# Two graph layers by two-level Strassen products on one core: the norms' shift on GpSimd, T1 of y out of PSUM, joint sums for P7 and P4, a last pair at full width, and new orders

## The chip, the cores and the metric

The kernel runs on one core of a Trainium2 chip. The time is device microseconds of that core, from one launch. A core has TensorE (PE in the profile, with PEld for its weight loads), VectorE (DVE), ScalarE (ACT), GpSimd (POOL) and SyncE (SP, which here issues every DMA). They run side by side, each in its own order, and meet through semaphores. SBUF is the working memory; PSUM, eight banks of 512 f32 columns by 128 partitions, takes the products.

## The reference

There are 64 graphs of 256 nodes with 512 features each, and an adjacency matrix for each graph, all f32.

```python
# layer 0
deg = sum(adj, -1);  agg = (adj @ x) / max(deg, 1e-6)
x = layernorm(x + relu(concat([x, agg], 2) @ W.T))
# layer 1
q, k = split(x @ Wqk);  v = x @ Wv
w = mask / sqrt(512) * sum(q * (adj @ (k * mask)), -1)      # one score a node
x = layernorm(x + softmax(w over the nodes) * v)
```

A layer norm takes mean and variance over the 512 features. In the kernel `(adj @ x) @ W2.T` becomes `adj @ (x @ W2.T)`, and the two weights of q and k are multiplied with each other once, so that a layer is one product of x with two weight blocks (own part and y, or q and v) and one product of the adjacency with a 256x512 matrix, the gather.

## The kernel before

Graphs are worked in pairs; `NP` is 32. All matmuls are f32. A matmul of 128x128 by n columns is two instructions in the profile.

**The outer products.** The product of a pair's x (transposed, `xT` for layer 0 and `x1T` for layer 1) with the weights is cut into 2x2 blocks and done with seven block products P1 to P7 instead of eight (Winograd's form). `outer_sums`, `fourth_sums` and `weight_sums` make the sums S1 to S4 of x and T1 to T4 of the weights. A product at full width (`outer`) is four matmuls of 512 columns for the pair.

**The inner products.** The products named in `INNER`, all but P6, are cut once more (`inner`, L551 on): seven matmuls of 256 columns. Their sums of x, four rows by three slots in the tile `xT_i` or `x1T_i`, are made by `inner_sums` on GpSimd (L512); `SLOTS_X` says which product uses which slot, and so which product has to be done before another's sums can be made. Each inner matmul lands in one half of a work bank `w`, and has to be taken out before that half is used again: ScalarE copies it to the small tile `fifth` or to the bank of the product, and VectorE adds it. These instructions stand in the profile as ACT `fifth<-bank` and DVE `bank<-bank,fifth`.

**The gather.** `sums_T` (L628) makes T1 to T4 of the 256x512 matrix, `adj_sums` the sums of the adjacency, and `gather` does seven products of two matmuls. In layer 0 its matrix is y, and the sums go to the tile `tv`; P3 ends in the bank y, and `r` in `layer0` copies it to SBUF, 512 columns for each graph of the pair, ahead of `sums_T`. `b11` and `b12` there are the two halves of that copy.

**The norms.** `norm_parts` (L708) gives three parts: ScalarE's mean and squares, then the factor (logarithm and exponential on ScalarE, then `shift = less * rstd`, 128x2, on VectorE), then ScalarE's `own<-own,shift,rstd`. Two norms a graph pair and layer, one for each graph.

**What sets the order.** The loop over pairs runs layer 0 of pair j beside layer 1 of pair j - 1. The order of the matmuls' groups is written out by letters: `ORDER0`, `ORDER1`, `ORDER` for j = 0, 1 and above, `ORDER9` for layer 1 of the last pair, which has no other pair beside it. Lower case is layer 0 and upper case layer 1: `i k m p q r s` and `J K H Q N P L` are products (i and J: P1; k and N: P5; m and K: P2; p and H: P6; q and Q: P7; r and L: P3; s and P: P4), `a` to `g` and `A` to `G` are gathers, and each letter stands for the next matmul group of its product. `HOME` and `HOME9` say which PSUM bank each of them works in. `take` (L890) walks the letters, and `when` starts other work, such as `inner_sums`, once given products are complete. Nothing is issued on the way: `Recorder` notes every operation in a `Plan`, and at the end `Plan.order` (L182) lists the steps of all five engines by a cost model, with due times that come from the place of the dependent matmuls in the letters. So an edit of a cost, an engine or a letter can move any instruction of any engine. Every operation of DVE, ACT and POOL has the line of the recorder, L285, and every matmul L370; they are told apart by their tiles.

**Pairs at the ends.** `FULL_FIRST` leaves P7 and P4 of layer 1 at full width for the first pair. After the loop the last pair's layer 1 runs alone, with `turn_here` for the transposes, `softmax_last` and two norms by halves.

Of the kernel before, what the change touches and what calls it, by code (L numbers as in the profile page):

```python
# [23 lines left out]


INNER = (("P1", "P2", "P5", "P3", "P4", "P7"), ("P1", "P2", "P5", "P3", "P4", "P7"))
SLOTS_X = {"P1": 0, "P2": 1, "P5": 2, "P3": 2, "P6": 0, "P7": 1, "P4": 0}
SLOTS_X1 = {"P1": 0, "P2": 1, "P5": 2, "P6": 0, "P7": 1, **({"P3": 2, "P4": 0} if "P7" in INNER[1] else {"P3": 0, "P4": 1})}
W1_BY_GP = ("P5", "P3", "P4")
HOME = "i6 k7 m7 p0 q6 r7 s6 a7 b2 c3 J3 K2 H5 Q5 N7 L6 P7 A6 B4 C5"  # L30
HOME9 = "J7 K6 H4 Q6 N7 L7 P0 A2 B3 C1"
LATE = 4.0
FULL_FIRST = ("P7", "P4")
ORDER0 = ("i k k i i i i i k i k k m m m k p m k p m p m m r p q r q q q r r r r q q r q s s s s s a b s s "
          "d e c f g")
ORDER1 = ("i k k i i k i k i k i i p m m k k m m p m m p p r r m q q r q r q q r q r q r s s s a J s J s s "
          "J s b J d J J e c J H f H K K H H K g Q K K K K Q N P C A N B Q D N E Q N G N F N N L L P L P L "
          "P L L")
ORDER = ("k k k k i i i L i i i i k m k p k m m p m m q r p p m r r m q q q q q q s s r r s r r s a J s J "
         "J s s b d e J g J c f J J K H K H K K H K K K H A N Q Q Q N Q N Q Q N D N C E Q F P P P G P B N "  # L40
         "P N L P L P L L L L")
ORDER9 = ("J J J J J J J C A D K K E B K K H F G K H Q N H N K H K N N N Q Q Q Q Q N Q P N L P P L L P P P "
          "L P S L Z L L")


class Step:
# [254 lines left out]
class Side:  # L301
# [11 lines left out]
    def chunk(self, s, k, e):  # L313
        return self.block(s)[:, k, e]

    def first_row(self, k, e):
        return self.a[:, k, :, e, 0]


@with_exitstack  # L320
def resnorm_kernel(
# [139 lines left out]
        mm(bank.rearrange("p (a n) -> p a n", n=P), ones,  # L461
           ones[:, None, :].to_broadcast([P, F // P, P]), start=True)

    waiting_sums = {}

    def weight_sums(w, name, layer, by_gp=()):
        b11, b21, b12, b22 = (w[:, k * H:(k + 1) * H, :] for k in range(4))
        t1, t2, t4 = (mem.tile([P, H, F], F32, name=f"{name}{k}") for k in (1, 2, 4))
        it = [mem.tile([P, len(INNER[layer]), HF], F32, name=f"{name}i{r}") for r in (1, 2, 4)]
        sides = {"P1": b11, "P2": b21, "P3": b22, "P4": t4, "P5": t1, "P6": t2, "P7": b12}  # L470
        sub = vec.tensor_sub

        def inner_of(p, b, later=None):
            later = layer == 1 and p in FULL_FIRST if later is None else later
            if p not in INNER[layer]:
                return
            n = INNER[layer].index(p)
            sub = gp.tensor_sub if p in by_gp else vec.tensor_sub
            c11, c12, c21, c22 = (b[:, e, h * HF:(h + 1) * HF] for e in range(2) for h in range(2))
            i1, i2, i4 = (i[:, n] for i in it)  # L480
            if later:
                waiting_sums[p] = lambda: inner_of(p, b, False)
                return
            sides[p] = {"B11": c11, "B21": c21, "B22": c22, "T3": c12, "T1": i1, "T2": i2, "T4": i4}
            sub(i1, c12, c11)
            sub(i2, c22, i1)
            sub(c12, c22, c12)
            sub(i4, c21, i2)
        sub(t1, b12, b11)
        inner_of("P1", b11)  # L490
        sub(t2, b22, t1)
        inner_of("P5", t1)
        sub(b12, b22, b12)
        sub(t4, b21, t2)
        inner_of("P2", b21)
        inner_of("P6", t2)
        inner_of("P7", b12)
        inner_of("P3", b22)
        inner_of("P4", t4)
        return sides  # L500
# [10 lines left out]

    def inner_sums(X, p, eng=gp):  # L512

        if p is None:
            a = [X.first_row(k, e) for k in range(2) for e in range(2)]
            i = [X.i[:, r, 0:2] for r in range(4)]
        else:
            a = [X.chunk(BLOCK[p], k, e) for k in range(2) for e in range(2)]
            i = [X.i[:, r, X.slots[p]] for r in range(4)]
        for to, op, c, d in ((i[0], OP.add, a[2], a[3]), (i[1], OP.subtract, i[0], a[0]),  # L520
                             (i[2], OP.subtract, a[0], a[2]), (i[3], OP.subtract, a[1], i[1])):
            eng.tensor_tensor(to, c, d, op=op)
# [105 lines left out]
    def sums_T(val, to=None):  # L628
        b11, b12, b21, b22 = (val[:, :, t, h * HF:(h + 1) * HF] for t in range(NT) for h in range(2))
        if to is None:  # L630
            tv = ring("tv", [P, 3, 2, HF])
            t1, t2, t4 = (tv[:, r] for r in range(3))
            t3 = b12
        else:
            t1, t2, t4, t3 = (to[:, :, t, h * HF:(h + 1) * HF] for t in range(NT) for h in range(2))
        vec.tensor_sub(t1, b12, b11)
        vec.tensor_sub(t2, b22, t1)
        vec.tensor_sub(t3, b22, b12)
        vec.tensor_sub(t4, b21, t2)
        return {"B11": b11, "B21": b21, "B22": b22, "T1": t1, "T2": t2, "T3": t3, "T4": t4}  # L640

# [63 lines left out]
                onto(1, 0, u)  # L705
        return dict(zip(names, ([u1], [g2], [g5], [u2], [u3], [g3], [u4])))

    def norm_parts(src, total, n=NT):  # L708
        rstd, shift, less, var = (small(x, [P, n]) for x in ("rstd", "shift", "less", "var"))

        def squares():
            act.activation(less, total, AF.Copy, scale=-1.0 / F)
            for t in range(n):
                junk = ring("junk", [P, F], 1, BF16)
                act.activation(junk, src[:, t], AF.Square, bias=less[:, t:t + 1], accum_out=var[:, t:t + 1])

        def factor():
            act.activation(rstd, var, AF.Ln, bias=eps, scale=1.0 / F)
            act.activation(rstd, rstd, AF.Exp, scale=-0.5)
            vec.tensor_tensor(shift, less, rstd, op=OP.mult)  # L720

        def scale(t):
            act.activation(src[:, t], src[:, t], AF.Identity, bias=shift[:, t:t + 1], scale=rstd[:, t:t + 1])
        return squares, factor, scale
# [115 lines left out]
    def layer0(j, X, o, u, y, at):  # L840

        own, yt = owns[j], ys[j]
        make = lambda p, w, q, done, onto=None: product(0, p, X, W0, w, q, done, onto)
        return {
            "i": make("P1", at["i"], u, lambda k: act.copy(own[:, k, 0], u[k])),
            "k": make("P5", at["k"], y, lambda k: act.copy(yt[:, k, 1], y[k])),
            "m": make("P2", at["m"], o, lambda k: act.copy(own[:, k, 0], o[k]), own[:, :, 0]),
            "p": make("P6", at["p"], u, lambda k: vec.tensor_add(yt[:, k, 0], u[k], yt[:, k, 1])),
            "q": make("P7", at["q"], u, lambda k: vec.tensor_add(yt[:, k, 1], u[k], yt[:, k, 1])),
            "r": make("P3", at["r"], y, lambda k: act.copy(yt[:, k, 0], y[k]), yt[:, :, 0]),  # L850
            "s": make("P4", at["s"], u, lambda k: act.copy(own[:, k, 1], u[k])),
        }

# [73 lines left out]
    for j in range(NP):  # L927
# [9 lines left out]
        def when(done, work):  # L937
            waiting.append((full(done, sizes), work))
# [34 lines left out]
            degrees(j + 1)  # L973
        when("k", lambda: (fourth_sums(X), x_sums("P3")))
        when("i", lambda: x_sums("P6"))
        when("m", lambda: x_sums("P7"))
        when("p" if "P6" in INNER[0] else "i", lambda: x_sums("P4"))
        when("pqr", start_gather0)
        when("rs", next_x)
        when("abcdefg", end_gather0)  # L980
# [2 lines left out]
        else:  # L983
# [29 lines left out]
                                    aggs[j - 1]))  # L1013
            when("L" if j > 1 else "m", start_layer1)
            when("J", lambda: y_sums("P6"))
            when("K", lambda: y_sums("P7" if "P7" in INNER[1] else "P4"))
            when("H", lambda: (fourth_sums(Y), y_sums("P4" if "P7" in INNER[1] else "P3")))
            if "P7" in INNER[1]:
                when("HN", lambda: y_sums("P3"))
            T = []  # L1020
            when("ikmpqrs" if j == 1 else "", lambda: T.append(sums_T(owns[j - 1], aggs[j - 1])))
            when("gK", start_gather1)
# [9 lines left out]
    X, x1 = x1Ts[j], owns[j]  # L1032
    turn_here(X, x1, 0, pf)
    take("L " * len(ahead), {"L": ahead}, Counter(), [])
    softmax(j - 1)
    aggs[j] = agg_of(j)
    T = sums_T(x1, aggs[j])
# [6 lines left out]
    at = homes(HOME9)  # L1044
    units, dots = layer1(j, X, q_at, o, u, y, at)
    units.update(gather("ABCDEFG", sumsM.pop(j), T, at["A"], at["C"], at["B"], aggs[j]))
    units["L"] = inner("P3", X, W1, at["L"], y, onto=vs[j][:, :, 0])
    last = []

    def sums(*ps):  # L1050
# [13 lines left out]
    def divide():  # L1064
# [1 line left out]
            last[k](pw[k])  # L1066

    units.update(S=[exps], Z=[divide])
    seven = "P7" in INNER[1]
    sizes = {name: len(parts) for name, parts in units.items()}  # L1070
    waiting = [(full(done, sizes), work) for done, work in (
        ("AB", lambda: (outer_sums(X, vec), sums("P5"))),
        ("J", lambda: sums("P6")),
        ("K", lambda: sums("P7" if seven else "P4")),
        ("H", lambda: (fourth_sums(X), sums("P4" if seven else "P3"))),
        ("HN", lambda: sums("P3") if seven else None),
        ("BFK", dots))]
    take(ORDER9, units, Counter(), waiting)
    p = small("probs", [P, 2, NT], 2)
# [10 lines left out]
    for k in range(2):  # L1090
        total = small("total2", [P, 1], 2)
        stt(k, 1, vs[j][:, k, 1], accum_out=total)
        squares, factor, scale = norm_parts(x1[:, k, 1:2], total, 1)
        squares()
        factor()
        scale(0)
# [34 lines left out]
```

## Time and profile before

| | |
|---|---|
| median of 3 runs | 1842.4 us (1842.38 to 1844.39) |
| profiled execution | 1842.84 us, span 1841.0 us |
| granted TensorE clock | 0.997 |
| PE busy | 1818.4 us, 99% of the span |
| DVE busy | 1672.4 us, 91% |
| ACT busy | 1332.0 us, 72% |
| POOL busy | 1269.4 us, 69% |
| DMA | 181.75 MB, mean 99 GB/s |

Busy time is the time in which an engine has an instruction; the rest of the span it waits. A row of a group names the line, the engine, the operation, the tile written and those read, the shapes, the count, and then the busy time and the mean duration of one. A row of a timeline begins with the start in microseconds from the span's start and the time taken, and ends, in brackets, with the idle time before it and what ended it. A row of a window gives its length and then, for each engine, busy time and number of instructions; then come the clock, the share of the DMA engines and GB/s. Matmuls overlap in the pipe, so their own durations say little, and their starts are what to compare.

### The profile page before, as it was taken

The page shows a single profiled execution, that of the slowest core. Times are in us where ns is not written, and L with a number is a line of the kernel's source. Part 1 is how long each engine was busy: PE and PEld are TensorE (multiplying, and loading weights), DVE is VectorE, ACT ScalarE, POOL GpSimd, SP SyncE. Part 2 cuts the span into 40 slices and gives each one's busy share as a digit, 9 for nine tenths or more (in the row PEclk, how much of TensorE's full clock was granted, in tenths as well). Part 3 has the DMA queues.
Part 4 walks back from the last instruction along what each step waited for, and adds up shares of the span by engine and source line. Part 5 has one row for each costly group of instructions (what it writes and reads, how often), then busy time and mean ns, then how long its engine had stood idle before and what let it go on. Part 6 is the DMA issues. An engine that isn't in the chain of part 4 may idle for free.

```text
span 1841.0 us, 28183 instructions
## 1 busy us (share of the span) xinstructions
PE 1818.4 (99%) x7754; PEld 1433.2 (78%) x7754; DVE 1672.4 (91%) x3627; ACT 1332.0 (72%) x3491; POOL 1269.4 (69%) x1864
## 2 busy tenths in 40 slices
PE   9999999999999999999999999999999999999996
PEld 5767878878778778778778788787787787787785
DVE  7888999999999999999999999999999999999986
ACT  3657876778766778767778767787667787677775
POOL 6876676766676866767766767666768667677652
PEclk9999999999999999999999999999999999999998
DMA  7133333443343343334333334433334333343311
GB/s 247 41 75 102 100 87 98 110 109 94 89 103 102 98 108 100 81 102 118 99 100 102 87 99 110 107 96 88 102 104 99 106 101 81 100 118 100 100 22 64
DMA packets 380733, 181.75 MB, mean 99 GB/s; under 512 B 263712, under 2 KB 345248, under 8 KB 380576
## 3 DMA queue, kind: packets, MB, share of 16 engines
q1 hardware_dynamic: 380576, 179.94, 36.1%
q8 instruction: 63, 1.03, 0.2%
q14 instruction: 94, 0.77, 0.1%
HBM read 114.35 MB, written 34.08 MB: 81 GB/s over the span
## 4 chain that ended last, share of the span: by engine, by line
PE 96%; DVE 2%; ACT 1%; DMA 0%; issue 0%; POOL 0%; SPq 0%; ACTq 0%; DVEq 0%
PE bank L370 96%; DVE own L285 1%; DMA shared<-wqk_t 0%; DVE bank L285 0%; ACT own L285 0%; SPq L386 0%; PE bank L376 0%; DVE tv L285 0%; DVE shared L285 0%; DVE y L285 0%; POOL xT_s L285 0%; DVE w L285 0%; DVE turn L285 0%; DVE x L285 0%; ACT adj L285 0%
## 5 line engine op out<-in xcount | busy, mean ns | idle before, releaser
L285 DVE TENSOR_TENSOR bank<-bank,fifth 128x256 f32<-128x256 f32 x886 | 394.6, 467 | 56.8 <-ACT fifth L285 28.9
L285 ACT COPY fifth<-bank 128x256 f32<-128x256 f32 x632 | 226.9, 376 | 249.0 <-PE bank L370 248.5
L370 PE MATMUL bank<-t_i,x1T_i 128*128 128x256 f32 x760 | 213.2, 382 | 0.4 <-DVE bank L285 0.3
L285 ACT COPY shared<-bank 128x512 f32<-128x512 f32 x314 | 182.4, 595 | 39.9 <-PE bank L370 35.7
L285 POOL TENSOR_TENSOR x1T_i<-x1T 128x256 f32<-128x256 f32 (+1 forms) x188 | 102.5, 552 | 154.9 <-PE bank L370 151.4
L370 PE MATMUL bank<-t_i,xT_i 128*128 128x256 f32 x768 | 205.6, 383 | 1.3 <-POOL xT_i L285 0.9
L285 POOL TENSOR_TENSOR sa<-adj 128x256 f32<-128x256 f32 x128 | 107.4, 839 | 143.1 <-ACT adj L285 136.5
L285 DVE SCALAR_TENSOR_TENSOR own<-bank,rdeg,own 128x256 f32<-128x256 f32 x384 | 170.6, 478 | 27.5 <-PE bank L370 23.9
L285 ACT COPY bank<-bank 128x256 f32<-128x256 f32 (+1 forms) x352 | 148.5, 423 | 62.8 <-DVE bank L285 32.6
L285 ACT ACTIVATE junk<-own,less 128x512 bf16<-128x512 f32 x254 | 185.2, 729 | 3.1
L285 ACT ACTIVATE own<-own,shift,rstd 128x512 f32<-128x512 f32 x254 | 186.7, 810 | 0.4 <-DVE shift L285 0.4
L370 PEld LDWEIGHTS bank<-t_i,xT_i 128*128 128x128 f32 x768 | 142.5, 189 | 43.4 <-ACT bank L285 8.9
L285 ACT COPY y<-bank 128x512 f32<-128x512 f32 x256 | 144.6, 588 | 40.8 <-PE bank L370 39.0
L370 PEld LDWEIGHTS bank<-t_i,x1T_i 128*128 128x128 f32 x760 | 139.9, 189 | 43.5 <-issue 16.1
L370 PE MATMUL bank<-t,x1T_s 128*128 128x512 f32 (+1 forms) x384 | 168.2, 521 | 0.0
L285 DVE TENSOR_TENSOR shared<-bank,shared 128x512 f32<-128x512 f32 (+1 forms) x157 | 140.8, 897 | 25.6 <-PE bank L370 23.1
L370 PE MATMUL bank<-t,xT_s 128*128 128x512 f32 (+1 forms) x384 | 163.5, 521 | 0.1
L370 PE MATMUL bank<-w,x1T_i 128*128 128x256 f32 x508 | 148.9, 384 | 3.1 <-DVE bank L285 1.7
L285 ACT COPY own<-bank 128x512 f32<-128x512 f32 x192 | 112.5, 587 | 47.7 <-PE bank L370 46.8
L370 PE MATMUL bank<-w,xT_i 128*128 128x256 f32 x512 | 143.0, 383 | 0.6 <-DVE bank L285 0.6
L285 POOL TENSOR_TENSOR xT_i<-xT 128x128 f32<-128x128 f32 (+1 forms) x188 | 103.0, 548 | 54.3 <-PE bank L370 42.7
L285 DVE SCALAR_TENSOR_TENSOR own<-own,x 128x512 f32<-128x512 f32 x128 | 131.8, 1033 | 0.0
(173 smaller groups left out, 4805.9 us busy)
## 6 DMA issues: line engine op xcount, KB each, us to landing
x<-x SPq DMA_DIRECT2D x64, 512.0 KB, 3.5
xT<-x_t SPq DMA_DIRECT2D x62, 512.0 KB, 3.5
out<-own SPq DMA_DIRECT2D x62, 512.0 KB, 3.8
x1T<-turn SPq DMA_DIRECT2D x480, 64.0 KB, 2.1
adj<-adj_t SPq DMA_DIRECT2D x64, 256.0 KB, 2.9
turn<-adj SPq DMA_DIRECT2D x64, 256.0 KB, 3.4
turn<-dram SPq DMA_DIRECT2D x31, 264.0 KB, 5.2
shared<-wqk_t SPq DMA_DIRECT2D x4, 512.0 KB, 8.2
```

The costliest lines, as they stand in the source:

```text
L285: self.plan.record(self.name, lambda: call(out, *args, **kwargs), outs, ins, busy, done, port)
L370: plan.record("PE", lambda: nc.tensor.matmul(ps, a, b, start=start, stop=True, skip_group_check=True), [ps], [a, b], busy, busy + 0.165, w ...
```

## The change

- `norm_parts` makes the shift on GpSimd; the last two half norms keep it on VectorE.
- `r` of layer 0 copies only the left half of each y on ScalarE, and VectorE subtracts this half from the right half in PSUM. So the right half of the tile holds T1 when `sums_T` begins, which then makes T2, T3 = T2 - B11 and T4, three subtractions instead of four.
- The sums for the inner products P7 and P4 are made together, four instructions of 256 columns instead of eight of 128. P7 moves to slot 0 and P4 to slot 1, next to each other, and both start when P1 and P2 are done. The first layer 1, with both at full width, has none.
- In the last pair's layer 1, P7, P4 and P3 are done at full width. Three subtractions on GpSimd give those weight blocks back. P3 adds onto the bank of P5, to which VectorE has added the part of v; `after_p5` takes the place of `add_p5`.
- The four orders and both tables of banks are new.

```diff
-SLOTS_X = {"P1": 0, "P2": 1, "P5": 2, "P3": 2, "P6": 0, "P7": 1, "P4": 0}
+SLOTS_X = {"P1": 0, "P2": 1, "P5": 2, "P3": 2, "P6": 0, "P7": 0, "P4": 1}
+SLOTS_X1 = SLOTS_X
-HOME = "i6 k7 m7 p0 q6 r7 s6 a7 b2 c3 J3 K2 H5 Q5 N7 L6 P7 A6 B4 C5"
-HOME9 = "J7 K6 H4 Q6 N7 L7 P0 A2 B3 C1"
+HOME = "i6 k7 m7 p2 q6 r7 s6 a7 b2 c3 J3 K2 H1 Q5 N7 L7 P7 A6 B4 C5"
+HOME9 = "J1 K7 H3 Q7 N6 L1 P1 A2 B3 C1"
+FULL_LAST = ("P7", "P4", "P3",)
-ORDER = ("k k k k i i i L i i i i k m k p k m m p m m q r p p m r r m q q q q q q s s r r s r r s a J s J "
-         "J s s b d e J g J c f J J K H K H K K H K K K H A N Q Q Q N Q N Q Q N D N C E Q F P P P G P B N "
-         "P N L P L P L L L L")
+ORDER = ("i k i i i k k i k i k i k m k p p p m m q m m r p r r m m r r r q q r q q q J q s J J s s s J J "
+         "s a b d s s J e c J H f K K H K H g K K H K K Q Q A N Q N Q Q D N N C Q Q N P N E P N P P G P P "
+         "P L F L B L L L L L")
...
-        if p is None:
-            a = [X.first_row(k, e) for k in range(2) for e in range(2)]
+        if p in (None, "P7P4"):
+            a = [X.row(k, e, int(p is not None)) for k in range(2) for e in range(2)]
...
-            t1, t2, t4 = (tv[:, r] for r in range(3))
-            t3 = b12
+            t2, t3, t4 = (tv[:, r] for r in range(3))
+            t1 = b12
...
+        if to is None:
+            vec.tensor_sub(t3, t2, b11)
+        else:
+            vec.tensor_sub(t3, b22, b12)
...
-            vec.tensor_tensor(shift, less, rstd, op=OP.mult)
+            by.tensor_tensor(shift, less, rstd, op=OP.mult)
...
+        def split(to, ps):
+            act.copy(to[:, :HF], ps[:, :HF])
+            vec.tensor_sub(to[:, HF:], ps[:, HF:], to[:, :HF])
-            "r": make("P3", at["r"], y, lambda k: act.copy(yt[:, k, 0], y[k]), yt[:, :, 0]),
+            "r": make("P3", at["r"], y, lambda k: split(yt[:, k, 0], y[k]), yt[:, :, 0]),
...
-        when("m", lambda: x_sums("P7"))
-        when("p" if "P6" in INNER[0] else "i", lambda: x_sums("P4"))
+        when("im", lambda: inner_sums(X, "P7P4"))
...
+    for p in FULL_LAST:
+        gp.tensor_sub(W1[p]["T3"], W1[p]["B22"], W1[p]["T3"])
+        W1[p] = whole[1, p]
...
+    def after_p5(k):
+        vec.tensor_add(v[:, k, 1], y[k], v[:, k, 1])
+        vec.tensor_add(y[k], y[k], v[:, k, 0])
+    units["N"] = product(1, "P5", X, W1, at["N"], y, after_p5)
+    units["L"] = [go for k in range(2) for go in outer(y, k, X, BLOCK["P3"], W1["P3"])]
```

More of the change, by code (lines that the diff above doesn't have):

```diff
@@ L26 @@
 INNER = (("P1", "P2", "P5", "P3", "P4", "P7"), ("P1", "P2", "P5", "P3", "P4", "P7"))
-SLOTS_X = {"P1": 0, "P2": 1, "P5": 2, "P3": 2, "P6": 0, "P7": 1, "P4": 0}
-SLOTS_X1 = {"P1": 0, "P2": 1, "P5": 2, "P6": 0, "P7": 1, **({"P3": 2, "P4": 0} if "P7" in INNER[1] else {"P3": 0, "P4": 1})}
+SLOTS_X = {"P1": 0, "P2": 1, "P5": 2, "P3": 2, "P6": 0, "P7": 0, "P4": 1}
+SLOTS_X1 = SLOTS_X
 W1_BY_GP = ("P5", "P3", "P4")
-HOME = "i6 k7 m7 p0 q6 r7 s6 a7 b2 c3 J3 K2 H5 Q5 N7 L6 P7 A6 B4 C5"
-HOME9 = "J7 K6 H4 Q6 N7 L7 P0 A2 B3 C1"
+HOME = "i6 k7 m7 p2 q6 r7 s6 a7 b2 c3 J3 K2 H1 Q5 N7 L7 P7 A6 B4 C5"
+HOME9 = "J1 K7 H3 Q7 N6 L1 P1 A2 B3 C1"
 LATE = 4.0
+FULL_LAST = ("P7", "P4", "P3",)
 FULL_FIRST = ("P7", "P4")
[L34 to L38, printed above, removed]
-ORDER = ("k k k k i i i L i i i i k m k p k m m p m m q r p p m r r m q q q q q q s s r r s r r s a J s J "
-         "J s s b d e J g J c f J J K H K H K K H K K K H A N Q Q Q N Q N Q Q N D N C E Q F P P P G P B N "
-         "P N L P L P L L L L")
-ORDER9 = ("J J J J J J J C A D K K E B K K H F G K H Q N H N K H K N N N Q Q Q Q Q N Q P N L P P L L P P P "
-          "L P S L Z L L")
+ORDER0 = ("k i i i k i i i i p k k k k m k p m m p q m m r m p m q q q q r q r r r q r s s s s s r s a s b "
+          "d e c g f")
+ORDER1 = ("i i k i k k k k k i i i i p m m k m p m m p p q m r r m q q q q r q r r r q s r s J a s J J J b "
+          "J s s s s d e c g J J f H K K H K K K N H N N K Q K C N N Q A D E B H Q N G P Q N P L P P L L L "
+          "F L L L")
+ORDER = ("i k i i i k k i k i k i k m k p p p m m q m m r p r r m m r r r q q r q q q J q s J J s s s J J "
+         "s a b d s s J e c J H f K K H K H g K K H K K Q Q A N Q N Q Q D N N C Q Q N P N E P N P P G P P "
+         "P L F L B L L L L L")
+ORDER9 = ("A J J J J J J J C K B D E H G H Q N Q N K H F H K N P Q K P Q K N K N N K P N L P S L L L Z")
 class Step:
@@ L314, in chunk, with row @@
         return self.block(s)[:, k, e]
-    def first_row(self, k, e):
-        return self.a[:, k, :, e, 0]
+    def row(self, k, e, v):
+        return self.a[:, k, :, e, v]
 @with_exitstack
@@ L462, in resnorm_kernel @@
            ones[:, None, :].to_broadcast([P, F // P, P]), start=True)
-    waiting_sums = {}
+    waiting_sums, whole = {}, {}
     def weight_sums(w, name, layer, by_gp=()):
@@ L483, in inner_of @@
                 return
+            whole[layer, p] = b
             sides[p] = {"B11": c11, "B21": c21, "B22": c22, "T3": c12, "T1": i1, "T2": i2, "T4": i4}
@@ L631, in sums_T @@
             tv = ring("tv", [P, 3, 2, HF])
-            t1, t2, t4 = (tv[:, r] for r in range(3))
-            t3 = b12
+            t2, t3, t4 = (tv[:, r] for r in range(3))
+            t1 = b12
         else:
             t1, t2, t4, t3 = (to[:, :, t, h * HF:(h + 1) * HF] for t in range(NT) for h in range(2))
-        vec.tensor_sub(t1, b12, b11)
+        if to is not None:
+            vec.tensor_sub(t1, b12, b11)
         vec.tensor_sub(t2, b22, t1)
-        vec.tensor_sub(t3, b22, b12)
+        if to is None:
+            vec.tensor_sub(t3, t2, b11)
+        else:
+            vec.tensor_sub(t3, b22, b12)
         vec.tensor_sub(t4, b21, t2)
@@ L706, in gather, with norm_parts @@
         return dict(zip(names, ([u1], [g2], [g5], [u2], [u3], [g3], [u4])))
-    def norm_parts(src, total, n=NT):
+    def norm_parts(src, total, n=NT, by=gp):
         rstd, shift, less, var = (small(x, [P, n]) for x in ("rstd", "shift", "less", "var"))
@@ L1015, in resnorm_kernel @@
             when("J", lambda: y_sums("P6"))
[L1016 to L1019, printed above, removed]
+            if j > 1:
+                when("JK", lambda: inner_sums(Y, "P7P4"))
+            when("H", lambda: fourth_sums(Y))
+            when("HN", lambda: y_sums("P3"))
             T = []
@@ L1046, in resnorm_kernel @@
     units.update(gather("ABCDEFG", sumsM.pop(j), T, at["A"], at["C"], at["B"], aggs[j]))
-    units["L"] = inner("P3", X, W1, at["L"], y, onto=vs[j][:, :, 0])
+    v = vs[j]
+    def after_p5(k):
[3 more added lines that the diff above has]
+    units["L"] = [go for k in range(2) for go in outer(y, k, X, BLOCK["P3"], W1["P3"])]
     last = []
@@ L1068, in resnorm_kernel @@
     units.update(S=[exps], Z=[divide])
-    seven = "P7" in INNER[1]
     sizes = {name: len(parts) for name, parts in units.items()}
@@ L1073, in resnorm_kernel @@
         ("J", lambda: sums("P6")),
-        ("K", lambda: sums("P7" if seven else "P4")),
-        ("H", lambda: (fourth_sums(X), sums("P4" if seven else "P3"))),
-        ("HN", lambda: sums("P3") if seven else None),
+        ("H", lambda: fourth_sums(X)),
         ("BFK", dots))]
@@ L1092, in resnorm_kernel @@
         stt(k, 1, vs[j][:, k, 1], accum_out=total)
-        squares, factor, scale = norm_parts(x1[:, k, 1:2], total, 1)
+        squares, factor, scale = norm_parts(x1[:, k, 1:2], total, 1, vec)
         squares()
```

## The prediction

> **What bounds the kernel now.** First I read busy times and slices on the page, then the waits of TensorE, then windows over three pairs, then timelines inside one pair, then the tail.
>
> ```profile
> PE 1818.4 (99%) x7754; PEld 1433.2 (78%) x7754; DVE 1672.4 (91%) x3627; ACT 1332.0 (72%) x3491; POOL 1269.4 (69%) x1864
> PEclk9999999999999999999999999999999999999998
> ```
>
> TensorE (PE) is the bound, at full clock, and VectorE (DVE) is next. So work taken from DVE, ScalarE (ACT) or GpSimd (POOL) is worth only the PE waits that it ends. Three successive pairs in the middle:
>
> ```profile
> 901.49:957.39 55.90, 55.90 (x242) 44.50 (x241) 51.66 (x113) 41.49 (x109) 39.41 (x59) 1.00 0.37 100
> 957.39:1013.30 55.91, 55.91 (x242) 44.51 (x241) 51.69 (x113) 41.49 (x109) 39.48 (x60) 1.00 0.37 100
> 1013.30:1069.20 55.90, 55.90 (x242) 44.50 (x241) 51.64 (x113) 41.49 (x109) 39.42 (x60) 1.00 0.38 100
> ```
>
> A pair takes 55.90 us. Successive unhindered PE starts are 0.216 us apart for 256 columns and 0.429 for 512 (a product is two instructions). A pair has 224 of the first (12 inner products of 7 and 28 gathers, twice) and 16 of the second: 224 x 0.2158 + 16 x 0.4292 = 55.2 us. Hence "busy" hides 0.69 us of lateness a pair. Summing this over the trace, PE loses 12.4 us before 200 us, 19 between 200 and 1750 (28 pairs), 5.7 from there to its end at 1828.9; then come 12.1 us without matmuls. Of the first 12.4, 1.9 are weight loads from HBM and about 2.2 the steady rate; 8.3 belong to the start.
>
> Where a pair loses it, seen on PE and then DVE:
>
> ```profile
> 938.33 0.59 PE L370 MATMUL bank<-w,x1T 128*128 128x256 f32 x2
> 938.85 0.67 PE L370 MATMUL bank<-t,x1T_i 128*128 128x256 f32 x2
> ...
> 936.09 1.72 POOL L285 TENSOR_TENSOR xT_s<-xT 128x512 f32<-128x512 f32 x1
> 937.00 1.35 DVE L285 SCALAR_TENSOR_TENSOR own<-own,x 128x512 f32<-128x512 f32 x1
> 938.29 0.42 DVE L285 TENSOR_TENSOR bank<-bank,fifth 128x256 f32<-128x256 f32 x1
> ```
>
> The matmul at 938.85 starts 0.10 us late, and the one behind it 0.075 late: it waited for the DVE add at 938.29, queued behind an `own<-own,x` that took 1.35 us (the same form takes 0.68 at 940.45) while POOL ran. Each pair has a second such wait (942.97: 0.10), two for ACT (939.85: 0.13; 957.39: 0.14), and 0.12 with no wait at all. So 0.27 a pair is late DVE, 0.27 late ACT.
>
> ```profile
> 942.73 0.52 DVE L285 TENSOR_TENSOR shift<-less,rstd 128x2 f32<-128x2 f32 x1
> 942.49 0.73 POOL L285 TENSOR_TENSOR xT_i<-xT 128x256 f32<-128x256 f32 x1
> ...
> L285 DVE TENSOR_TENSOR shift<-less,rstd 128x2 f32<-128x2 f32 x126 | 54.2, 431 | 0.0
> ```
>
> Two columns cost DVE 0.52 us and end, at 943.25, just after the POOL instruction (943.22). Beside no POOL work the same shift takes 0.15. A two-input DVE instruction in SBUF waits for the running POOL instruction.
>
> **What the Trainium skill says.** GPSIMD Engine Reference, 8 Key points: POOL shares its SBUF interfaces with DVE and contends with DVE instructions of two SBUF inputs; the 0.52 against 0.15 agrees. TensorE: Matmul & The Clock Gate, Part 2: weight loads are pulled ahead, matmuls keep program order, so one late operand holds all; the second 0.075 at 939.14, with no wait of its own, agrees.
>
> **The change, part by part.** Sums start from the profiled execution, 1842.84 us, 1.84 over its span of 1841.0; the median of the runs, 1842.4, is 0.4 lower.
>
> *Shift on GpSimd.* DVE loses 126 x 0.431 = 54.2 us, about 1.75 a pair. POOL gains four a pair. Its rows are 0.46 us at 128 columns and 0.73 at 256, so 0.19 at zero: 4 x 0.19 = 0.76 (an estimate; no such POOL form is shown). From below it could be as short as DVE's 0.13, from above it queues behind one POOL instruction (1.70 for `xT_s<-xT`). POOL idles 16.5 us of a pair, which hides it. New wait: ACT's scale now waits for POOL, and behind that scale on ACT stand copies `fifth<-bank`, for which PE waits. Before, the use came 0.24 to 4.0 us after the shift's end, so I take no cost.
>
> *T1 out of PSUM.* Per pair DVE drops `tv<-y` (1.119) and adds two 128x256 subtractions out of PSUM (0.427 each for `bank<-bank,y`): -0.27. T3 now comes from T2, one for one. ACT copies 256 instead of 512 columns twice: 2 x (0.588 - 0.376) = -0.42. The bank stays occupied until the subtraction, some 0.2 us longer; other products cover that, and uncovered it is 0.2 x 28 = 5.6 us.
>
> *Sums for P7 and P4 together.* POOL, layer 0: eight of 0.46 to 0.48 (3.76) become four of 0.73 (2.92): -0.84; layer 1 likewise -0.85. With the shifts, -0.9 a pair. PE rarely waits for POOL, so directly nothing; indirectly DVE meets POOL less. P7 may start no earlier than P1 and P2 both allow; both are done long before.
>
> DVE goes from 51.7 to 49.6 us a pair. I take the late-DVE waits as ended and those for ACT, and the waitless rest, as staying: 28 x 0.27 = -7.5. Bounds: all waits end, -0.54 x 28 = -15; or the new orders restore them elsewhere, 0, or worse.
>
> *Last pair at full width.* PE gains, per product, 8 x 0.4292 - 14 x 0.2158 = 0.41, so +1.24. DVE loses for P7 and P4 3 x 0.43 + 0.69 plus one 0.43, twice (4.8), for P3 2.2, and the new adds behind P5 take 4 x 0.69 instead of 2 x 1.22 (+0.3): -6.7. ACT loses eight copies, -3.0. The three weight subtractions, about 0.8 us each, and dropped sums are on a POOL busy below half there. In the tail:
>
> ```profile
> 1822.48 0.70 PE L370 MATMUL bank<-t_i,x1T_i 128*128 128x256 f32 x2 [0.28 <-DVE bank L285]
> 1825.85 0.67 PE L370 MATMUL bank<-w,x1T_i 128*128 128x256 f32 x2 [1.33 <-DVE bank L285]
> ...
> 1832.92 1.50 ACT L285 ACTIVATE own<-own,shift,rstd 128x512 f32<-128x512 f32 x2
> ```
>
> PE loses 3.4 us there to adds of P4 and P3 (1821.5, 1822.5, 1825.9). In their place P3 waits for two adds behind P5 (1.4), partly under P4: 1.0. Net -3.4 + 1.0 + 1.24 = -1.2. After PE's end ACT still does the scale of pair 30, late because DVE was full; two scales and a root, 1.8 us, move forward: tail -3.0, between 0 and -5.
>
> *New orders and banks.* The matmuls stay the same but for the last pair; the order decides which evacuation is late. In the start, waits for DVE run from 45.75 (`tv`, 0.58 us, the very chain of T1) to 132; I take a bit over a third of 8.3: -3, between +3 and -7. No DMA is added or moved past another queue by the edits themselves; the load of the next x waits for the last P4, which the new order places later; at 37% DMA that is hidden.
>
> Sum: -3 - 7.5 - 3.0 = -13.5: 1829.3, as a median 1829.
>
> **The rivals.** (A) Above: 1829, chance 0.42. (B) Steady waits only change place; ends gain 6: 1836, 0.17. For it: ACT's waits are as large as DVE's. Against: DVE gets 2.1 us a pair. (C) Nearly all waits vanish: -15 - 7 - 4, 1816, 0.17. For it: DVE and POOL both get room. Against: unwaited lateness stays. (D) Slower: the shift queues behind a long POOL instruction, ACT stands, and its copies come late to PE. At 0.2 us reaching PE for each of 126 shifts, +25.2 - 13.5: 1854, 0.19. It decides from (13.5 + 3.7)/126 = 0.14 us each. For it: POOL instructions last up to 1.7 us and ACT is in order. Against: up to 4 us of distance before. (E) No net effect: 1842, 0.05.
>
> **How the numbers follow.** A measurement here tells 0.2%, 3.7 us, from nothing. Faster: A, C and 0.13 of B, 0.72. Same: the rest of B, E, 0.02 of D: 0.11. Slower: 0.17. Range 1814 to 1850 leaves out half of D (0.10) and C's lower third (0.06). A alone spans 1823 to 1834.
>
> **What would show it.** DVE busy near 1603 (1672.4 - 54.2 - 32 x 0.27 - 6.7), no `shift` row of 126 on DVE; POOL shifts near 0.19 us; a steady pair near 55.6 us; `tv<-y` gone; the last pair's matmuls with 512 columns and PE ending near 1817; under 11 us behind it. I am wrong if a pair takes 56.1 us or more: then ACT idles for POOL, or PE waits for ACT.

## The result

The changed kernel takes 1822.3 us (median of 4 runs, 1821.68 to 1822.29) against 1842.6 us before (1842.38 to 1844.39). The ratio is 0.9887, with a 95% interval of 0.987 to 0.9904: 20 us less, where the prediction had 13.5 and the range 1814 to 1850.

First the busy times on the page of the changed kernel, then two pairs in its middle and the page's row of the shift (the columns are as before):

```profile
PE 1804.1 (99%) x7736; PEld 1441.2 (79%) x7736; DVE 1569.2 (86%) x3521; ACT 1300.2 (71%) x3483; POOL 1201.2 (66%) x1733
```

```profile
903.92:959.27 55.35, 55.35 (x241) 44.88 (x240) 48.27 (x110) 40.52 (x110) 37.30 (x55) 1.00 0.38 101
959.27:1014.62 55.35, 55.35 (x242) 44.99 (x241) 48.32 (x110) 40.52 (x110) 37.37 (x55) 1.00 0.39 102
```

```profile
L285 POOL TENSOR_TENSOR shift<-less,rstd 128x2 f32<-128x2 f32 x126 | 23.6, 206 | 215.1 <-ACT rstd L285 213.6
```

A pair has come from 55.90 us to 55.35 us, and its matmuls alone need 55.2: the waits inside the pairs are nearly gone, those for ACT as well as those for DVE. DVE has lost 103 us, where the prediction had counted 69 for what is taken from it (1672 to 1603 us). Part of the rest is that instructions which stay meet less of POOL's work: the 128 of `own<-own,x` come from a mean of 1.03 us to 0.88. The shift takes 0.2 us on POOL.

The ledger below is made as in the prediction: the distances between successive starts of PE, less 0.2158 us for 256 columns and 0.4292 us for 512, summed over a stretch. The last two rows are not lateness but work and the time without matmuls.

| us | before | after | difference | predicted |
|---|---|---|---|---|
| PE late, 0 to 200 us | 12.4 | 11.3 | -1.2 | -3 |
| PE late, 200 to 1750 us | 19.7 | 5.9 | -13.8 | -7.5 |
| PE late, from 1750 us to PE's end | 5.7 | 3.0 | -2.7 | -2.4 |
| full width in the last pair | | | +1.24 | +1.24 |
| from PE's end to the end of the span | 12.1 | 8.0 | -4.1 | -1.8 |
| span | 1841.0 | 1820.5 | -20.5 | -13.5 |

The tail, in the timeline of the changed kernel: PE meets one wait of the kind that cost 3.4 us before. Pair 30's last scale on ACT (1808.30) now runs ahead of PE's end at 1812.5, where two of its scales stood at 1832.9 before, behind PE's end; ACT's last scale (1815.41) belongs to the last pair itself.

```profile
1807.37 1.10 PE L370 MATMUL bank<-w,x1T_s 128*128 128x512 f32 x2 [0.57 <-DVE bank L285]
1808.30 0.80 ACT L285 ACTIVATE own<-own,shift,rstd 128x512 f32<-128x512 f32 x1
1815.41 0.80 ACT L285 ACTIVATE own<-own,shift,rstd 128x512 f32<-128x512 f32 x1
```

### The profile page after: what moved, and what is told of

It reads as the page before. It is cut to its first block, busy times and chain, and to the rows that moved or that the text cites. A ratio compares the mean times of both kernels' runs of the same rounds, so it can differ in the third digit from the quotient of the medians.

```text
span 1820.5 us, 27950 instructions
## 1 busy us (share of the span) xinstructions
PE 1804.1 (99%) x7736; PEld 1441.2 (79%) x7736; DVE 1569.2 (86%) x3521; ACT 1300.2 (71%) x3483; POOL 1201.2 (66%) x1733
## 3 DMA queue, kind: packets, MB, share of 16 engines
q8 instruction: 63, 1.03, 0.3%
## 4 chain that ended last, share of the span: by engine, by line
PE 97%; DVE 1%; ACT 1%; DMA 1%; SPq 0%; issue 0%; POOL 0%; ACTq 0%; DVEq 0%
PE bank L370 96%; DMA shared<-wqk_t 1%; DVE bank L285 0%; DVE own L285 0%; ACT own L285 0%; PE bank L376 0%; ACT junk L285 0%; DVE y L285 0%; SPq L386 0%; ACT turn L285 0%; ACT fifth L285 0%; ACT adj L285 0%; DVE turn L285 0%; DVE tv L285 0%; POOL shift L285 0%
## 5 line engine op out<-in xcount | busy, mean ns | idle before, releaser
L285 DVE TENSOR_TENSOR bank<-bank,fifth 128x256 f32<-128x256 f32 (+1 forms) x876 | 381.5, 464 | 118.8 <-ACT fifth L285 80.3
L285 ACT COPY y<-bank 128x512 f32<-128x512 f32 (+1 forms) x256 | 135.0, 532 | 117.0 <-PE bank L370 99.9
L370 PE MATMUL bank<-t_i,x1T_i 128*128 128x256 f32 x748 | 208.2, 379 | 1.5 <-ACT bank L285 1.5
L285 ACT ACTIVATE own<-own,shift,rstd 128x512 f32<-128x512 f32 x254 | 200.6, 828 | 2.4 <-POOL shift L285 2.2
L370 PE MATMUL bank<-t_i,xT_i 128*128 128x256 f32 x768 | 197.8, 380 | 0.1
L285 DVE TENSOR_TENSOR y<-bank,y 128x512 f32<-128x512 f32 (+1 forms) x256 | 150.4, 618 | 23.8 <-PE bank L370 22.2
L285 POOL TENSOR_TENSOR shift<-less,rstd 128x2 f32<-128x2 f32 x126 | 23.6, 206 | 215.1 <-ACT rstd L285 213.6
L285 POOL TENSOR_TENSOR x1T_i<-x1T 128x256 f32<-128x256 f32 x124 | 97.6, 797 | 74.0 <-PE bank L370 72.1
L285 POOL TENSOR_TENSOR xT_s<-xT,xT_s 128x256 f32<-128x256 f32 x62 | 64.0, 1048 | 110.1 <-PE bank L370 108.6
L285 POOL TENSOR_TENSOR sa<-adj 128x256 f32<-128x256 f32 x128 | 92.7, 733 | 58.5 <-ACT adj L285 53.9
```

What stands on the lines that cost most here:

```text
L285: self.plan.record(self.name, lambda: call(out, *args, **kwargs), outs, ins, busy, done, port)
L370: plan.record("PE", lambda: nc.tensor.matmul(ps, a, b, start=start, stop=True, skip_group_check=True), [ps], [a, b], busy, busy + 0.165, w ...
```

## The experiments

Two theories for the steady pairs. "Room", the one of the prediction: DVE was too full, and its waits behind POOL made PE wait. "Orders" or "list": what counts is the order in which the planner lists every engine's instructions, and the new letters give a better one.

### One part at a time, listed anew

```diff
 e1_old_orders: the changed kernel, with HOME, ORDER0, ORDER1 and ORDER of before
 e2_shift_dve: the changed kernel
-    def norm_parts(src, total, n=NT, by=gp):
+    def norm_parts(src, total, n=NT, by=vec):
 e3_new_orders_only: the kernel before, with the new HOME, ORDER0, ORDER1 and ORDER
 e4_shift_only: the kernel before (the last two half norms pass vec)
-    def norm_parts(src, total, n=NT):
+    def norm_parts(src, total, n=NT, by=gp):
...
-            vec.tensor_tensor(shift, less, rstd, op=OP.mult)
+            by.tensor_tensor(shift, less, rstd, op=OP.mult)
```

> The changed kernel with the old HOME, ORDER0, ORDER1 and ORDER (the last pair's order stays new). Theory 'room' (the steady waits ended because VectorE gets 2 us a pair and its waits behind GpSimd go): most of the gain stays, 1827 us or less, a steady pair at most 55.5 us. Theory 'orders' (the letters and banks decide which evacuation is late): the steady waits come back, 0.5 us or more a pair, 1835 to 1840 us.

> The changed kernel with the shift of the norms back on VectorE, all else new. 'Room': VectorE is back to about 51.3 us a pair, the waits return at 0.3 us a pair or more, 1831 us or more. 'Orders': within 4 us of the changed kernel, 1822 to 1826 us.

> The kernel before with the new HOME, ORDER0, ORDER1 and ORDER alone. 'Room': no gain beyond the start, 1839 us or more, perhaps slower than before, since these orders count on the freed VectorE. 'Orders': half of the steady gain or more, 1835 us or less.

> The kernel before with the shift on GpSimd alone, old orders. 'Room': VectorE loses 1.7 us a pair and the two VectorE waits a pair end: 1835 us or less. 'Orders': 1839 to 1843 us. The slower rival of the prediction (ScalarE stands behind a shift that queues on GpSimd) would show here as over 1846 us and as idle time of ScalarE before own<-own,shift,rstd.

| run | us | ratio to before (95%) | DVE busy, us | PE late, 200 to 1750 us |
|---|---|---|---|---|
| before | 1842.6 | | 1672 | 19.7 |
| after | 1822.3 | 0.987 to 0.9904 | 1569 | 5.9 |
| e1_old_orders | 1868.3 | 1.0123 to 1.0154 | 1619 | 48.2 |
| e2_shift_dve | 1859.9 | 1.0076 to 1.0109 | 1606 | 39.8 |
| e3_new_orders_only | 1888.7 | 1.0233 to 1.0264 | 1644 | 62.4 |
| e4_shift_only | 1858.9 | 1.0068 to 1.0098 | 1606 | 35.0 |

Neither theory has all four. Every part of the change is slower than both kernels, by 16 to 46 us against before, and in each DVE is *less* busy than before. Room falls as it was put, although e2 and e3 lie in the ranges that it gave: e4 frees 66 us of DVE and loses 16 us, and e1 should have kept most of the gain. Orders falls too, if it says that the new letters are better by themselves: e3 is the slowest of the four. The time of e4 lies where the slower rival of the prediction was to show (over 1846 us), but its mechanism isn't there. In e4's waits, for ACT and for PE (us in total, times, longest), ACT hardly stands for the shift, and PE waits elsewhere:

```profile
ACT own L285 <- POOL shift L285: 1.0, 3, 0.4
```

```profile
PE bank L370 <- DMA x1T<-turn: 6.0, 21, 0.3
PE bank L370 <- DVE bank L285: 5.7, 12, 0.9
```

What the four have in common is that one edit makes a wholly new list. Between e2 and the changed kernel one argument differs; compared line by line, about three tenths of the instructions of PE and of DVE and four tenths of ACT's stand at another place of their list. So an edit is measured here together with a new list for it, and letters fitted to other costs. The two have to be taken apart.

### The list kept

In the next runs the planner still counts what it counted in the parent kernel, and only what is issued at a place of the list is changed. For e5 and e6 the lists of PE, ACT and SP are the parent's, line for line, and those of DVE and POOL differ in the shifts alone.

```diff
 e5_list_kept_shift_pool: the kernel before
+    listed = Recorder(plan, "DVE", nc.gpsimd, vec_cost)     # listed as before, issued on GpSimd
 e6_list_kept_shift_dve: the changed kernel
+    listed = Recorder(plan, "POOL", nc.vector, gp_cost)     # listed as after, issued on VectorE
 e7_list_kept_sums_apart: the changed kernel, each joint sum of P7 and P4
+                tc.keep_in_program_order(nc.gpsimd.tensor_tensor(to[:, 0], c[:, 0], d[:, 0], op=op))
+                return nc.gpsimd.tensor_tensor(to[:, 1], c[:, 1], d[:, 1], op=op)
```

> The kernel before, its instruction list kept on every engine, with only the 126 shifts issued on GpSimd instead of VectorE at the same places. 'Room' (VectorE's load and its waits behind GpSimd set the steady waits): VectorE loses 1.7 us a pair and the time falls to 1837 us or less. 'List' (what counts is how the planner's list fits the costs; the engine of one small instruction is worth little): 1838 to 1844 us. The slower rival of the prediction (ScalarE stands behind a shift that queues on GpSimd): over 1847 us, with ScalarE idle before own<-own,shift,rstd.

> The changed kernel, its instruction list kept, with only the 126 shifts issued on VectorE. 'Room': the VectorE waits return, 1831 us or more. 'List': 1821 to 1827 us, in contrast to the 1859.9 us of the run that let the planner make a new list for the same edit.

> The changed kernel, its list kept, with each joint sum for P7 and P4 issued as two GpSimd instructions of 128 columns: 1.7 us more of GpSimd a pair and more meetings with VectorE. 'Room': 0.1 us or more a pair, 1826 us or more. 'List': under 1824 us, since GpSimd has 17 us a pair to spare.

**e5: 1841.6 us, ratio 0.9994 (0.9985 to 1.0002).** DVE's busy time falls by 43 us to 1629 us, POOL's shift takes 0.196 us, and nothing is gained: 18.5 us of lateness between 200 and 1750 us, after 19.7. The timeline of e5 at the very wait that the prediction meant to end:

```profile
936.86 0.59 PE L371 MATMUL bank<-w,x1T 128*128 128x256 f32 x2
937.39 0.67 PE L371 MATMUL bank<-t,x1T_i 128*128 128x256 f32 x2
...
934.62 1.72 POOL L285 TENSOR_TENSOR xT_s<-xT 128x512 f32<-128x512 f32 x1
935.54 1.35 DVE L285 SCALAR_TENSOR_TENSOR own<-own,x 128x512 f32<-128x512 f32 x1
936.82 0.42 DVE L285 TENSOR_TENSOR bank<-bank,fifth 128x256 f32<-128x256 f32 x1
```

It is the picture of before. The matmul at 937.39 is 0.10 us late, behind an add that stands behind the same `own<-own,x` of 1.35 us. That instruction meets a sum of the next pair's x on POOL, and no shift has a part in it: the shifts stood further down DVE's list, and what they leave free lies behind this add. e4 has the very same instructions as e5 on every engine, only in another order, and takes 17 us more; so it is e4's list that made it slow, not the shift on POOL.

**e6: 1832.8 us (ratio 0.9931 to 0.996), 10.6 us slower than the changed kernel.** The time lies where room had put it (1831 us or more), but not for its reason, that the waits of the steady pairs return. From 400 to 1600 us PE is late by 0.35 to 0.7 us in 200, as in the changed kernel, although DVE makes every shift again. The same 1200 us in the kernel before, in e6 and in e2 (DVE is the third of the five engines):

```profile
400.00:1600.00 1200.00, 1200.00 (x5155) 955.38 (x5154) 1108.38 (x2403) 886.74 (x2332) 849.71 (x1249) 1.00 0.38 100
400.00:1600.00 1200.00, 1200.00 (x5201) 973.54 (x5200) 1063.04 (x2453) 875.42 (x2360) 793.56 (x1082) 1.00 0.39 101
400.00:1600.00 1200.00, 1190.36 (x5074) 940.49 (x5073) 1048.10 (x2390) 869.85 (x2297) 770.48 (x1056) 1.00 0.37 99
```

DVE keeps most of its room in e6, 1063 us busy against 1108, so e6 alone doesn't rule room out. Together with e2 it does: e2 has the very same instructions as e6 on every engine, in another order, and its DVE is no busier. PE is late there by 32.2 us in these 1200, in e6 by 2.9. So the list decides, and the steady pairs don't need the shift on POOL once the list is this one.

The loss of e6 is in the start (3.3 us more by 200 us), between 200 and 300 us (2.5 us more), and around 1727 us. There, in e6's timelines of DVE, POOL and PE and then in windows of PE's clock (the figure behind the five engines):

```profile
1723.27 2.65 DVE L285 TENSOR_TENSOR shift<-less,rstd 128x2 f32<-128x2 f32 x2
...
1722.49 1.29 POOL L285 TENSOR_TENSOR xT<-xT 128x512 f32<-128x512 f32 x1
1723.72 1.43 POOL L285 TENSOR_TENSOR sa<-adj 128x256 f32<-128x256 f32 x2
1725.08 0.74 POOL L285 TENSOR_TENSOR sa<-sa,adj 128x256 f32<-128x256 f32 x1
...
1726.73 1.10 PE L371 MATMUL bank<-t_i,x1T_i 128*128 128x256 f32 x4 [2.25 <-DVE bank L285]
```

```profile
1728.40:1731.50 3.10, 3.10 (x8) 2.47 (x8) 2.30 (x5) 2.77 (x5) 0.00 (x0) 0.51 0.37 100
```

The first of two shifts of two columns takes 2.575 us on DVE: it starts at 1723.27 and ends with the last of four POOL instructions that run back to back. Everything on DVE stands behind it, PE idles for 2.25 us, and soon after runs 3 us at half clock. Most of the loss in the start is half clock too: from 98.6 to 103.5 us the granted clock is 0.52, behind waits of 1.2 and 1.6 us. The four runs of e6 spread over 4 us, and the profiled one is the slowest. What the shift on POOL is worth on this list is the freedom from such accidents at the ends, about 10 us, and nothing in the steady pairs.

**e7: 1824.2 us (ratio 0.9888 to 0.9918), 1.9 us slower.** The joint sums are worth that much on this list. All of it lies between 200 and 1750 us (7.9 us late instead of 5.9), but again none from 400 to 1600 us. It is two waits close together near the end, of the same kind as e6's:

```profile
1741.13 4.44 DVE L285 TENSOR_TENSOR tv<-y 128x512 f32<-128x512 f32 x1
...
1741.27 1.29 POOL L285 TENSOR_TENSOR x1T<-x1T 128x512 f32<-128x512 f32 x1
1742.50 1.29 POOL L285 TENSOR_TENSOR x1T_s<-x1T_s,x1T 128x512 f32<-128x512 f32 x1
1743.72 0.89 POOL L285 TENSOR_TENSOR x1T_i<-x1T_s 128x128 f32<-128x128 f32 x2
1744.54 0.48 POOL L285 TENSOR_TENSOR x1T_i<-x1T_i,x1T_s 128x128 f32<-128x128 f32 x1
...
1745.63 0.70 PE L370 MATMUL bank<-tv,sa 128*128 128x256 f32 x2 [0.91 <-DVE tv L285]
1747.50 0.70 PE L370 MATMUL bank<-w,x1T_i 128*128 128x256 f32 x2 [1.17 <-DVE bank L285]
```

T2 (`tv<-y`) takes 4.44 us beside five POOL instructions without a gap. In the changed kernel the same two engines meet at 1742.03, but there T2 starts ahead of `x1T<-x1T` and takes 0.71 us, and it is the POOL instruction that takes 1.71 us instead of 1.29.

### T1 of y, with the list kept

```diff
 shortened: the calls issued at the kept places, without the lines that record them
 e10_list_kept_T1_sbuf: the changed kernel, at the places of the copy and of the subtraction
-            act.copy(to[:, :HF], ps[:, :HF])
-            vec.tensor_sub(to[:, HF:], ps[:, HF:], to[:, :HF])
+            nc.scalar.copy(to, ps)
+            nc.vector.tensor_sub(right, right, left)
 e12_list_kept_T1_sbuf: the changed kernel, all pairs but the first
-            vec.tensor_sub(to[:, HF:], ps[:, HF:], to[:, :HF])
+            nc.scalar.copy(right, ps[:, HF:])                    # listed at the same place
...
+                tc.keep_in_program_order(nc.vector.tensor_sub(t1, b12, b11))
                 return nc.vector.tensor_sub(t2, b22, t1)         # T1 in front of T2
```

> The changed kernel, its list kept, with T1 of y out of SBUF: ScalarE copies all 512 columns of y at the place where it copied 256, and VectorE makes T1 from the copy, in place, at the place of the subtraction out of PSUM. VectorE then reads two SBUF inputs and can meet GpSimd. If T1 out of PSUM matters for itself, 0.1 us a pair or more is lost: 1825 us or more. If it mattered only through the list that it allowed: 1821 to 1824 us.

> The changed kernel, its list kept, with T1 of y made as before: for every pair but the first, ScalarE copies the right half of y too, at the place where VectorE subtracted out of PSUM, and VectorE makes T1 with one 512 column subtraction of two SBUF inputs, in front of T2. ScalarE gains 0.75 us a pair, VectorE changes by -0.86 and +0.7 to 1.2 us, and T1 is ready later by up to 1 us. If T1 out of PSUM ends a wait of PE by itself, the steady pairs lose 0.1 us or more each: 1826 us or more. If it is worth something only through the list: 1821 to 1825 us.

e10 took 1845.2 us (ratio 1.0004 to 1.0022), but it isn't the experiment that it was meant to be: the whole copy stands where the list has the left half's, at which the right half of y need not be complete, so that its T1 is not the reference's and its waits are not those of the edit. e12 was made in its place, with the right half copied where it is complete.

**e12: 1854.7 us, ratio 1.0065 (1.0048 to 1.0082), 32 us slower than the changed kernel.** PE's lateness between 200 and 1750 us goes from 5.9 to 32.3 us. It is one wait in each pair, here in e12's timelines of DVE and PE:

```profile
926.73 0.99 DVE L641 TENSOR_TENSOR y<-y 128x512 f32<-128x512 f32 x1 [0.97 <-ACT y L861]
927.75 1.64 DVE L642 TENSOR_TENSOR tv<-y 128x512 f32<-128x512 f32 x1
929.32 0.47 DVE L285 SCALAR_TENSOR_TENSOR own<-bank,rdeg,own 128x256 f32<-128x256 f32 x1
...
929.85 0.70 PE L370 MATMUL bank<-y,adj 128*128 128x256 f32 x2 [0.56 <-DVE own L285]
```

DVE waits 0.97 us for ACT's second copy, makes T1 in 0.99 us and T2 in 1.64 us (both have two SBUF inputs; POOL works beside most of the first and all of the second), and only then comes to `own<-bank,rdeg,own`, which empties the bank that the gather's next matmul needs. That matmul is 0.72 us late, and the next one 0.10. So T1 out of PSUM, to which the prediction gave no worth on PE's path in the steady pairs, is the one edit of the three tried on this list whose loss shows in every pair. The run also puts T1 later than a list made for it might; it says what the edit is worth here, not what a kernel without it could reach.

### The last pair

```diff
 e8_last_inner and e9_last_inner_list_kept: the changed kernel, with the old ORDER9 and HOME9
-    for p in FULL_LAST:
-        gp.tensor_sub(W1[p]["T3"], W1[p]["B22"], W1[p]["T3"])
-        W1[p] = whole[1, p]
...
-    units["N"] = product(1, "P5", X, W1, at["N"], y, after_p5)
-    units["L"] = [go for k in range(2) for go in outer(y, k, X, BLOCK["P3"], W1["P3"])]
+    units["L"] = inner("P3", X, W1, at["L"], y, onto=vs[j][:, :, 0])
 e9_last_inner_list_kept: also, in Plan.order
+                    if number[s] < self.kept and number[s] != kept[e][-1]:
+                        continue            # steps ahead of the last layer 1 in the changed kernel's order
```

> The changed kernel with P7, P4 and P3 of the last pair as inner products again, with the old ORDER9 and HOME9 and the old additions behind P5. The steady pairs and the start stay. By the prediction's sum 3.0 us are lost: 1825 us. By the two traces (7 us less in the tail) up to 1829 us. If the last pair's width is nothing and the tail came from an earlier norm of pair 30, 1822 to 1823 us.

> As e8_last_inner, but all steps up to the last pair's layer 1 keep the changed kernel's instruction list; only the steps of that layer are listed anew, with the old ORDER9 and HOME9. If e8's 77 us came from a new list of the steady pairs, this one has steady pairs without waits and is 2 to 8 us slower than the changed kernel: 1825 by the prediction's sum (3.0), 1828 by what the tail gained between the two traces (5.6). If the inner products of the last pair cost the 77 us themselves, it is over 1880 us.

e8 takes 1898.9 us (ratio 1.0289 to 1.0323). An edit of the last of 64 layers makes all pairs slower: 68.9 us late between 200 and 1750 us, with DVE busy for only 1582 us. The due times are computed backwards from the program's end (`Plan.latest`), so even the steady pairs are listed anew. e9 has the very same instructions as e8 on every engine, with the list of the steady pairs kept, and takes 1830.9 us (0.9921 to 0.995). Its start and its steady pairs are those of the changed kernel (11.0 and 5.9 us late), and all of its 8.6 us lies in the tail: PE late by 8.9 instead of 3.0 us, 12.3 instead of 8.0 us behind PE's end, less the 1.24 us of work. The longest of PE's waits in e9:

```profile
PE bank L908 <- DVE w L361: 2.4, 1, 2.4
```

PE waits for the scores of the softmax, which stand on DVE behind other work, the inner products' adds among it.

### A search of letters

The planner has an end of its own, the time at which its cost model sees the last step done. It is 1825.8 us for the kernel before and 1817.8 for the changed one, 1830 for e1, 1840 for e2, 1846 for e4, 1856 for e3 and 1892 for e8. That is not the measured order in all places, nor the measured size, but every run above that is slower than both kernels and was listed anew is slower by the planner too. So letters of ORDER and ORDER9 were moved about until this end was 3.9 us earlier.

```diff
-ORDER = ("... r r q q r q q q J q s J J s s s J J s a b d s s J e c J H f ...")
+ORDER = ("... r r q q r q q J q q s s s J J s J s a J b d s s e c J J H f ...")
-ORDER9 = ("A J J J J J J J C K B D E H G H Q N Q N K H F H K N P Q K P Q K N K N N K P N L P S L L L Z")
+ORDER9 = ("J J J J A J J D C J B E K G H H Q K N N Q F K H H N P K N Q K K N Q P K N P N L P L L S Z L")
```

> The changed kernel with a few letters of ORDER (from q to e) and many of ORDER9 moved, so that the planner's own end is 3.9 us earlier. The steady pairs have almost no waits left to lose, so a gain can come only from the ends, where PE still loses 14 us: 1818 to 1823 us. If the fit of the list to the chip is as fragile as the runs so far say, the steady waits come back: over 1826 us.

**e11: 1817.9 us (1817.2 to 1819.37), ratio 0.9866 (0.9851 to 0.9881).** It is the fastest kernel of the study, 4.3 us below the changed one; the intervals of the two ratios overlap, the runs do not. The steady pairs keep 6.0 us of lateness. The start has 7.7 instead of 11.3 us, the tail 2.5 instead of 3.0, and 7.6 us come behind PE's end instead of 8.0.

## Why the prediction was right and where it failed

**Right in direction and range, by a wrong step.** The step that failed is "I take the late-DVE waits as ended", from DVE's 2 us of room. e5 gives DVE most of that room on the old list (1.4 us a pair), and both DVE waits of a pair stay. What the runs show in its place is the list: in e4 and e5, in e2 and e6, and in e8 and e9 the same instructions in another order differ by 17, 27 and 68 us. The same step has "those for ACT, and the waitless rest, as staying"; ACT's went too, and with it the size: -13.8 us and not -7.5. The steady pairs came out as in rival C, the ends nearer to B. How the 13.8 us divide between T1 out of PSUM and the new letters stays open: no run has the one without the other on a list as well fitted.

That the whole came out faster was in part luck. The prediction let an edit be counted by itself and gave "slower" 0.19, for a shift that queues. The parts listed anew were all slower, by 16 to 46 us, through lists that didn't fit, and nothing in the prediction's sum tells a fitting list from another.

**The shift.** The cost was right: 0.19 us estimated for POOL, 0.195 measured as the median, and the 54.2 us on DVE gone. That ACT would wait for it was rightly given no cost: 2.2 us of ACT's idle time in all, so the mechanism of the slower rival is not there. But e4 against e5 shows that the edit can be slower all the same, by a way that no rival had: a new list from letters made for other costs.

**T1.** The durations were right (0.415 us for a subtraction out of PSUM, 0.427 taken), and "other products cover that" held for the bank: PE is late by more than 0.03 us only once in a steady pair of the changed kernel, by 0.07 us. What the sum left out in the steady pairs is the chain from y's bank to the next gather; it counted the edit as 0.27 us of DVE alone. e12 lengthens this chain on the new list, and PE loses 0.82 us to it in every pair.

**Joint sums.** "Directly nothing" is right for the steady pairs. The 1.9 us of e7 come from one meeting of DVE and POOL near the end.

**The second delay of a wait.** The 0.075 us at 939.14 was read as program order at work. Order alone lets the second matmul start 0.216 us behind the first, and it started 0.291 us behind, as others do behind a wait. What adds the 0.075 us isn't shown.

**The last pair.** PE's 1.24 us are as computed, 7736 instructions instead of 7754. The term for PE's waits was near (-2.7 against -2.4). The time behind PE's end was undersized: two scales and a root were counted as moving forward, 1.8 us, while 4.1 us went. With its letters, e9 puts the whole part at 8.6 us, against 3.0 in the sum.

**The start.** -3 was a guess at a third of 8.3 us, and -1.2 came: the waits of 0.9 and 1.1 us by 51 and 64 us are smaller, and one of 1.7 us by 99 us is new. e11 shows that 3.6 us more are to be had there.

**What would show it.** A pair near 55.6 us (55.35), DVE near 1603 us (1569: instructions that stayed got shorter as well), PE's end near 1817 us (1812.5), under 11 us behind it (8.0).

## What to carry to other kernels

Where one order for all engines is made by a planner from costs, an edit and the list that it causes are two changes: keep the list and change only what is issued, and then change the list, before crediting either (the same instructions differ by 68 us in e8 and e9, by 27 us in e2 and e6). How busy an engine is says little about who is late: with DVE busy for 1582 us in e8, PE was 68.9 us late between 200 and 1750 us, and with 1569 us in the changed kernel 5.9. A removed instruction was worth here what its chain cost at the next bank that had to come free, not its duration.

## What the runs showed of the hardware

- A VectorE instruction of two columns with two SBUF inputs took 0.13 to 0.15 us alone, 0.52 beside one POOL instruction, and 2.575 us beside four that followed one another without a gap: it didn't come in between them, it ended with the last. In e7 a subtraction of 512 columns, 0.71 us in the changed kernel, took 4.44 us beside five. GPSIMD Engine Reference, 8 Key points, in the Trainium skill speaks of contention; that a DVE instruction can stand through a whole run of POOL's is what e6 and e7 add.
- POOL's fixed cost is small: 0.195 us for 128x2, against 0.46 for 128 columns and 0.73 for 256.
- After 2.25 us without a matmul, PE ran for about 3 us at a granted clock of 0.51, beginning 1.7 us after it had started again; eight instructions of 256 columns took 0.43 us each instead of 0.216. TensorE: Matmul & The Clock Gate, Part 1, in the skill gives half clock as the idle state, after an idle window of about 3.4 us; here the gap was shorter. So the wait of 2.4 us cost about 4. Two waits of 1.9 and 2.0 us by 1540 us of e1 were followed by half clock as well, and one of 2.6 us by 1878 us of e8 was not: in these runs the length of a gap alone doesn't decide it, and what does is not shown.
